# Issuing a batch's four input loads in two pairs, with the residual load and the probability stores between them

## The chip, the core and the metric

The kernel runs on one core of a Trainium2 chip. A core has a matrix engine (TensorE, PE in the profile, with its weight loads as PEld), a vector engine (VectorE, DVE), an activation engine (ScalarE, ACT), a general engine (GpSimd, POOL) and a queue engine (SyncE, SP), each with its own program, in order. They synchronise through semaphores. Transfers between the chip's memory (DRAM) and the on-chip memory run on 16 DMA engines. The metric is the time of one execution on the device in microseconds (us); lower is better.

## The reference, cut to what matters

The input x has 32 batches of 512 queries with 640 channels. The context has 77 keys per batch with 1024 channels. The text keys alone reach the attention that counts; there are 20 heads of 32 channels:

```python
residual = hidden_states
end = N_TXT                                    # 77
ehs_txt = encoder_hidden_states[:, :end]
...
q = _heads(hidden_states @ to_q_w)
h_txt = _sdpa(q, _heads(ehs_txt @ to_k_w), _heads(ehs_txt @ to_v_w))
...
out = _merge(h_txt) + SCALE_OBJ * _merge(h_obj) + SCALE_OTH * _merge(h_oth) + SCALE_IP * _merge(h_ip)
out = out @ to_out_w + to_out_b
out = (out + residual) / RESCALE               # RESCALE is 1
```

The context of this case has exactly 77 rows, so the slices for the object, other and image keys are empty, and their softmax over no keys adds zero. What is left is a cross attention of x to the context, a projection, a bias and the residual x, all in float32.

## The kernel before, in words

Matmuls take their float32 operands as a high and a low part (the high part is a copy in a narrower format, the low part the difference), and run three products: high by high, high by low, low by high. The function `split` and its relatives make the two parts: ScalarE copies, VectorE or GpSimd subtracts.

A first stage (up to line 252) computes all keys and values from the context and stores them in DRAM (`k_dram`, `v_dram`), and the split output weights in `wo_dram`. Then the main part runs 160 *slots*, one for each batch b and each group j = 0..4 of four heads, n = 5b + j. The order of all instructions of the main part is written out by hand (`tc.manual_schedule`), so each engine executes in the order of the program's text. `slot(n)` does, in this order and for quarters t = 0..3 of the queries:

- `refill`: loads of keys or values for later slots, on SP: in j=0 the keys of groups 2 to 4 (L309, L312), in j=1 and j=3 values (L319), in j=2 the next batch's keys.
- `cast_p`, `rest_p`, `last_p`: the probabilities of slot n-3, loaded from DRAM into `raw` one slot earlier, are split on ScalarE (L431, L437), VectorE (L438) and GpSimd (L445) into `pp`.
- `scores(n, t)` on TensorE (L367) with the maximum on VectorE (L375), and `exps(n, t)` on ScalarE (L385).
- `normalize(n-1)`: GpSimd scales the probabilities of the slot before in place (L400), behind the reciprocals of VectorE (L395).
- `queries(n+1)` on TensorE (L332), `split_q(n+1)` on ScalarE (L343, L347) and VectorE (L349).
- `load_p(n-2)` on SP (L423, L424): transposed probabilities back from DRAM into `raw`.
- `transpose_p(n-1)`: VectorE transposes blocks of 32x32 from `pn` into `z` (L407), and SP stores `z` to a DRAM tile `pd` with four transfers (L414). The tile `z` has one buffer, so the transposition of a slot waits until the stores of the slot before have landed.
- `values(n-3)` on TensorE (L459), and two `piece`s of the output projection (L489) of an earlier batch, whose results VectorE adds to bias and residual (`finish`, L517) and SP stores (L521).

Beside that, every batch's x is brought in. `load_x` loads it into the tile `xs`, which has one buffer, by four transfers of 32 partitions each (L267; 512 pieces of 640 bytes). They are issued on SP in slot j=4 of batch b for batch b+2. In slots j=0, 1 and 2 of the next batch VectorE transposes `xs` in place in four parts (`transpose_x`, L272), each of which reads all 128 partitions, so the first needs all four transfers. In slots j=2 and 3 `split_x` makes the parts `xt` of the query matmuls (L279, L280). The residual is loaded a second time, in the layout of the output (`load_residual`, L478), in slots j=1 to 4.

All transfers of the main part are issued by SP in program order. In slot j=4 that order is: two loads into `raw`, four loads of x, one load of the residual, four stores of `z`, one store of the output. Slot j=0 then begins with four loads of keys (kb, kc, kb, kc), two loads into `raw`, four more loads of keys and four stores of `z`.

Of the kernel before, what the change touches and what calls it, by code (L numbers as in the profile page):

```python
# [8 lines left out]
F32 = mybir.dt.float32  # L9
# [14 lines left out]
P = 128  # L24
Q = 32
# [25 lines left out]
def kernel(  # L51
# [26 lines left out]
    B, S, C = x.shape  # L78
# [176 lines left out]
    main = ctx.enter_context(tc.tile_pool(name="main", bufs=1, reuse_waits="tile"))  # L255
# [3 lines left out]

    xts, raws, pps, ats, xss, pds, sms, pqs, pas, xrs, pos = ({} for _ in range(11))  # L260

    def load_x(b):

        xs = main.tile([P, S // Q, C // 4], F32, tag="xs", name="xs")
        src = x[b].rearrange("(a j) (q u) -> q j a u", j=Q, q=4)
        for q in range(4):
            nc.sync.dma_start(xs[q * Q : (q + 1) * Q, :, :], src[q])  # L267
        xss[b] = xs

    def transpose_x(b, i):  # L270
        part = xss[b][:, 4 * i : 4 * i + 4, :].rearrange("p a u -> p (a u)")
        nc.vector.transpose(part, part)  # L272
# [53 lines left out]
    def queries(n, k0, k1):  # L326
        b, j = divmod(n, NC_)
        if k0 == 0:
            pqs[n] = ps.tile([P, S], F32, tag="pq", name="pq", bufs=1)
        for k in range(k0, k1):  # L330
            for m, (a, c) in enumerate(PAIRS):
                nc.tensor.matmul(  # L332
                    pqs[n],
                    wq_s[:, k, a, j * P : (j + 1) * P],
                    xts[b, k][:, c, :],
                    start=(k == 0 and m == 0),
                    stop=(k == NC_ - 1 and m == 2),
                )
# [14 lines left out]
    def scores(n, t):  # L353
        b, j = divmod(n, NC_)
        g = GROUP_OF[j]
        qt, (kb, kc) = qts[n % 2], kbs[g]
        jg = j - GROUPS[g][0]
        sc = ps.tile([P, S], F32, tag="sc", name="sc", bufs=3)
        half = KCOLS // 2
        for m, (cols, keys_) in enumerate(  # L360
            (
                (slice(0, KCOLS), kb[:, jg]),
                (slice(0, half), kc[:, jg, 0]),
                (slice(half, KCOLS), kc[:, jg, 1]),
            )
        ):
            nc.tensor.matmul(  # L367
                sc[:, cols],
                qt[:, m, t * P : (t + 1) * P],
                keys_,  # L370
                start=(m == 0),
                stop=(m == 2),
            )
        nm = main.tile([P, HPC], F32, tag="nm", name="nm", bufs=3)
        nc.vector.tensor_reduce(  # L375
            nm, sc[:, :KCOLS].rearrange("p (h k) -> p h k", k=NKEY), AX.X, ALU.max, negate=True
        )
        return sc, nm

    def exps(n, t, sc, nm):  # L380
        if t == 0:
            sms[n] = main.tile([P, NQ * HPC], F32, tag="sm", name="sm", bufs=2)
        for i in range(HPC):
            at = t * HPC + i
            nc.scalar.activation(  # L385
                pnb[n % 2][:, at, :NKEY],
                sc[:, i * NKEY : (i + 1) * NKEY],
                AF.Exp,
                bias=nm[:, i : i + 1],
                accum_out=sms[n][:, at : at + 1],  # L390
            )

    def sums(n):
        rs = main.tile([P, NQ * HPC], F32, tag="rs", name="rs", bufs=2)
        nc.vector.reciprocal(rs, sms.pop(n))  # L395
        return rs

    def normalize(n, rs):
        pf = pnb[n % 2][:, :, :NKEY]
        nc.gpsimd.tensor_tensor(  # L400
            pf, pf, rs.unsqueeze(2).to_broadcast([P, NQ * HPC, NKEY]), ALU.mult
        )
# [17 lines left out]
    def load_p(n):  # L420
        pd = pds.pop(n)
        raw = late[0].tile([P, 3, S], F32, tag="raw", name="raw", bufs=2)
        nc.sync.dma_start(raw[:, 0:2, :], pd[0 : 2 * P, :].rearrange("(k p) q -> p k q", p=P))  # L423
        nc.sync.dma_start(raw[:64, 2, :], pd[2 * P :, :])  # L424
        raws[n] = raw

    def cast_p(n):

        raw = raws[n]
        pp = late[0].tile([P, 5, S], FPR, tag="pp", name="pp", bufs=1)  # L430
        nc.scalar.copy(pp[:, 0:2, :], raw[:, 0:2, :])  # L431
        pps[n] = pp

    def rest_p(n):

        raw, pp = raws[n], pps[n]
        nc.scalar.copy(pp[:64, 4, :], raw[:64, 2, :])  # L437
        nc.vector.tensor_tensor(  # L438
            pp[:, 2:4, :], raw[:, 0:2, :], pp[:, 0:2, :].bitcast(F32), ALU.subtract
        )  # L440

    def last_p(n):

        raw, pp = raws.pop(n), pps[n]
        nc.gpsimd.tensor_tensor(  # L445
            pp[64:, 4, :], raw[:64, 2, :], pp[:64, 4, :].bitcast(F32), ALU.subtract
        )
# [27 lines left out]
    def load_residual(b, t, xr=None):  # L475
        if xr is None:
            xr = late[0].tile([P, C], F32, tag="xr", name="xr", bufs=3)
        nc.sync.dma_start(xr, x[b, t * P : (t + 1) * P, :])  # L478
        xrs[b, t] = xr

    def add_bias(b, t):
        nc.gpsimd.tensor_tensor(xrs[b, t], xrs[b, t], bias, ALU.add)  # L482
# [28 lines left out]
    def finish():  # L511

        while closed:
            b, t, h = closed.pop(0)
            xr = xrs[b, t]
            cols = slice(h * HALF, (h + 1) * HALF)
            nc.vector.tensor_tensor(  # L517
                xr[:, cols], pos.pop((b, t, h))[:, :HALF], xr[:, cols], ALU.add
            )
            if h == 1:  # L520
                nc.sync.dma_start(out[b, t * P : (t + 1) * P, :], xr)  # L521
# [21 lines left out]
    def refill(b, j, part):  # L543

        heads = range(2 * part, 2 * part + 2)
        segments = SEGMENTS[4 * part : 4 * part + 4]
        if j == 0:
            load_keys(b, 1, heads)
        elif j == 1:
            load_values(b, 0, segments)  # L550
        elif j == 2 and b + 1 < B:
            load_keys(b + 1, 0, heads)
        elif j == 3:
            load_values(b, 1, segments)

    def slot(n, beside=None):
        b, j = divmod(n, NC_)
        ahead, more = n + 1 < N, b + 1 < B
        back, first = PIECES[j]
        bo_, has_out = b - back, b >= back  # L560
        xsplits = SPLIT_X.get(j, ((), ())) if more else ((), ())
        turns = TRANSPOSE_X.get(j, ((), (), ())) if more else ((), (), ())
        taken, second = takes.get(n), seconds.get(n)

        refill(b, j, 0)
        if taken is not None:
            cast_p(taken)
        s = scores(n, 0)
        if taken is not None:
            rest_p(taken)  # L570
        if n:
            normalize(n - 1, sums(n - 1))
        if taken is not None:
            last_p(taken)
        exps(n, 0, *s)
        if ahead:
            queries(n + 1, 0, 2)
        s = scores(n, 1)
        if n - LAG + 1 in pds and n > LATE:
            load_p(n - LAG + 1)  # L580
        refill(b, j, 1)
        finish()
        if j == 4 and b + 2 < B:
            load_x(b + 2)
        if j in RESIDUAL and b >= RESIDUAL[j][0]:
            load_residual(b - RESIDUAL[j][0], RESIDUAL[j][1])
        if j in BIAS and b >= BIAS[j][0]:
            add_bias(b - BIAS[j][0], BIAS[j][1])
        exps(n, 1, *s)
        for i in turns[0]:  # L590
            transpose_x(b + 1, i)
        if ahead:
            queries(n + 1, 2, NC_)
        s = scores(n, 2)
        if n:
            transpose_p(n - 1)
        if ahead:
            split_q(n + 1)
        exps(n, 2, *s)
        for c in xsplits[0]:  # L600
            split_x(b + 1, c)
        if has_out:
            piece(bo_, first)
        if taken is not None:
            values(taken)
        if beside:
            beside()
        s = scores(n, 3)
        finish()
        for i in turns[1]:  # L610
            transpose_x(b + 1, i)
        if taken is not None:
            split_a(taken)
        for c in xsplits[1]:
            split_x(b + 1, c)
        exps(n, 3, *s)
        if has_out:
            piece(bo_, first + 1)
        for i in turns[2]:
            transpose_x(b + 1, i)  # L620
        if second is not None:
            cast_p(second)
            rest_p(second)
            last_p(second)
            take(second)
            if second + 2 in pds and second + 2 not in takes.values():
                load_p(second + 2)
# [141 lines left out]
```

## Time and profile before

| | us |
|---|---|
| three executions | 2025.39, 2026.93, 2027.08; median 2026.93 |
| the profiled execution | 2018.67, of which the span 2016.9 |
| TensorE busy in the span | 1963.4 (97%) |
| ScalarE, VectorE, GpSimd busy | 1588.0 (79%), 1354.7 (67%), 981.9 (49%) |
| DMA: 421.10 MB on SP's queue | 82.4% of the 16 engines' time |
| x loads, issue to landing | 7.5 median, 3.9 to 10.8 |
| z stores (`pd<-z`), issue to landing | 3.6 median |

How to read it: "L407 z" is the instruction of line 407 that writes tile z. In a row of a timeline the first number is the start in us from the span's start, the second the duration, and the brackets give the idle time of the engine before it and what ended that. In a row of waits the numbers are the total in us, how many times, and the longest. In a row of DMA issues they are the number of transfers, the size of one in KB, and the median time from issue to landing. The chain of work goes back from the last instruction, at each step to what released it. Idle time of an engine that isn't on the path to the end costs nothing.

### The profile page before, as it was taken

The page shows a single profiled execution, that of the slowest core. Times are in us where ns is not written, and L with a number is a line of the kernel's source. Part 1 is how long each engine was busy: PE and PEld are TensorE (multiplying, and loading weights), DVE is VectorE, ACT ScalarE, POOL GpSimd, SP SyncE. Part 2 cuts the span into 40 slices and gives each one's busy share as a digit, 9 for nine tenths or more (in the row PEclk, how much of TensorE's full clock was granted, in tenths as well). Part 3 has the DMA queues.
Part 4 walks back from the last instruction along what each step waited for, and adds up shares of the span by engine and source line. Part 5 has one row for each costly group of instructions (what it writes and reads, how often), then busy time and mean ns, then how long its engine had stood idle before and what let it go on. Part 6 is the DMA issues. An engine that isn't in the chain of part 4 may idle for free.

```text
span 2016.9 us, 38271 instructions
## 1 busy us (share of the span) xinstructions
PE 1963.4 (97%) x11012; PEld 1763.5 (87%) x11012; DVE 1354.7 (67%) x2159; ACT 1588.0 (79%) x6377; POOL 981.9 (49%) x617
## 2 busy tenths in 40 slices
PE   9999997899999999999999999999999999999998
PEld 7889986789888988888898888888888888988898
DVE  4443225777777777777777677777777777777764
ACT  3321128889889988888898899899898889989993
POOL 0000023555555555555556555666555655555554
PEclk9999998999999999999999999999999999999999
DMA  7993366888888888888988888888888888888875
GB/s 172 221 255 108 105 148 151 222 222 221 223 223 220 226 218 226 217 218 218 229 226 220 208 227 229 222 223 218 217 222 219 218 224 218 228 222 222 222 202 169
DMA packets 555997, 423.55 MB, mean 210 GB/s; under 512 B 170191, under 2 KB 459501, under 8 KB 555789
## 3 DMA queue, kind: packets, MB, share of 16 engines
q1 hardware_dynamic: 555789, 421.10, 82.4%
q8 instruction: 91, 1.49, 0.3%
q14 instruction: 117, 0.96, 0.1%
HBM read 245.61 MB, written 175.32 MB: 209 GB/s over the span
## 4 chain that ended last, share of the span: by engine, by line
PE 54%; DMA 19%; SPq 8%; POOL 6%; issue 5%; ACT 4%; DVE 4%; DVEq 0%; POOLq 0%; ACTq 0%
PE pq L332 17%; PE po L489 15%; DMA pd<-z 8%; PE pa L459 8%; PE sc L367 6%; POOL pn L400 4%; PE pv L197 4%; PE pk L168 4%; DMA xs<-in_x_dram 3%; DMA raw<-pd 3%; SPq L414 2%; DVE qt L349 2%; ACT pn L385 2%; POOL pp L445 2%; DMA kb<-k_dram 1%
## 5 line engine op out<-in xcount | busy, mean ns | idle before, releaser
L385 ACT ACTIVATE pn<-sc,nm 128x77 f32<-128x77 f32 x2560 | 799.2, 329 | 109.3 <-DVE nm L375 96.5
L400 POOL TENSOR_TENSOR pn<-pn,rs 128x1232 f32<-128x1232 f32 x160 | 364.5, 2278 | 692.6 <-DVE rs L395 541.2
L489 PE MATMUL po<-wo_s,at 128*128 128x320 f32 x3840 | 627.6, 313 | 1.4 <-DVE xr L517 1.4
L332 PE MATMUL pq<-xt,wq_s 128*128 128x512 f32 x2400 | 622.5, 400 | 0.0
L489 PEld LDWEIGHTS po<-wo_s,at 128*128 128x128 f32 x3840 | 567.0, 189 | 2.0 <-DVE xr L517 1.7
L385 ACT ACTIVATION_READ_ACCUMULATOR pn<-sc,nm 128x1 f32 x2560 | 530.6, 207 | 0.0
L332 PEld LDWEIGHTS pq<-xt,wq_s 128*128 128x128 f32 x2400 | 429.7, 190 | 77.5 <-POOL xt L280 0.2
L375 DVE TENSOR_REDUCE nm<-sc 128x4 f32<-128x308 f32 x640 | 294.0, 460 | 264.3 <-PE sc L367 258.1
L459 PE MATMUL pa<-pp,vb 128*128 128x512 f32 x1280 | 337.7, 402 | 19.6 <-ACT pp L431 9.9
L407 DVE STREAM_TRANSPOSE z<-pn 128x1280 f32<-128x1280 f32 x160 | 241.8, 1511 | 119.2 <-DMA pd<-z 62.4
L459 PEld LDWEIGHTS pa<-pp,vb 128*128 128x128 f32 x1280 | 242.5, 197 | 68.3 <-POOL pp L445 20.7
L367 PEld LDWEIGHTS sc<-kc,qt 128*128 128x128 f32 x1280 | 213.3, 189 | 40.9 <-issue 13.9
L367 PE MATMUL sc<-kc,qt 128*128 128x154 f32 x1280 | 227.1, 256 | 13.6 <-DVE qt L349 12.9
L438 DVE TENSOR_TENSOR pp<-raw,pp 128x1024 fp32r<-128x1024 f32 x160 | 196.2, 1226 | 50.1 <-ACT pp L431 34.3
L445 POOL TENSOR_TENSOR pp<-raw,pp 64x512 fp32r<-64x512 f32 x160 | 209.4, 1309 | 36.4 <-ACT pp L437 24.3
L349 DVE TENSOR_TENSOR qt<-pq,qt 64x512 fp32r<-64x512 f32 x320 | 214.3, 670 | 7.5 <-ACT qt L343 3.1
L280 POOL TENSOR_TENSOR xt<-xs,xt 128x512 fp32r<-128x512 f32 x157 | 199.7, 1299 | 16.8 <-ACT xt L279 12.2
L482 POOL TENSOR_TENSOR xr<-xr,bias 128x640 f32<-128x640 f32 x128 | 201.2, 1573 | 12.0 <-POOL pp L445 2.7
L347 ACT CAST qt<-qt 64x512 fp32r<-64x512 f32 x320 | 198.1, 619 | 9.0
L367 PE MATMUL sc<-kb,qt 128*128 128x308 f32 x640 | 196.0, 306 | 1.2 <-ACT qt L343 1.2
L431 ACT CAST pp<-raw 128x1024 fp32r<-128x1024 f32 x160 | 170.1, 1063 | 1.3 <-DVE at L105 0.8
L104 ACT CAST at<-pa 128x512 fp32r<-128x512 f32 x160 | 94.9, 593 | 75.5 <-PE pa L459 72.8
(41 smaller groups left out, 1536.3 us busy)
## 6 DMA issues: line engine op xcount, KB each, us to landing
pd<-z SPq DMA_DIRECT2D x640, 160.0 KB, 3.6
raw<-pd SPq DMA_DIRECT2D x160, 512.0 KB, 4.1
xs<-in_x_dram SPq DMA_DIRECT2D x128, 320.0 KB, 7.5
xr<-in_x_dram SPq DMA_DIRECT2D x128, 320.0 KB, 3.8
out_dram<-xr SPq DMA_DIRECT2D x128, 320.0 KB, 3.3
raw<-pd SPq DMA_DIRECT2D x160, 128.0 KB, 4.2
v_dram<-vs SPq DMA_DIRECT2D x19, 640.0 KB, 4.0
k_dram<-ks SPq DMA_DIRECT2D x80, 128.0 KB, 2.4
```

The lines of the kernel that those rows point to most:

```text
L280: engine.tensor_tensor(parts[1], src, parts[0].bitcast(F32), ALU.subtract)
L332: nc.tensor.matmul(pqs[n], wq_s[:, k, a, j * P : (j + 1) * P], xts[b, k][:, c, :], start=(k == 0 and m == 0), stop=(k == NC_ - 1 and m == 2),)
L349: nc.vector.tensor_tensor(qt[r, 1 + w, :], pq[r], qt[r, 0, :].bitcast(F32), ALU.subtract)
L367: nc.tensor.matmul(sc[:, cols], qt[:, m, t * P : (t + 1) * P], keys_, start=(m == 0), stop=(m == 2),)
L375: nc.vector.tensor_reduce(nm, sc[:, :KCOLS].rearrange("p (h k) -> p h k", k=NKEY), AX.X, ALU.max, negate=True)
L385: nc.scalar.activation(pnb[n % 2][:, at, :NKEY], sc[:, i * NKEY : (i + 1) * NKEY], AF.Exp, bias=nm[:, i : i + 1], accum_out=sms[n][:, at : ...
L400: nc.gpsimd.tensor_tensor(pf, pf, rs.unsqueeze(2).to_broadcast([P, NQ * HPC, NKEY]), ALU.mult)
L407: nc.vector.transpose(z.rearrange("p b t j -> p t b j"), pn.rearrange("p (t h) k -> p t (h k)", t=NQ).rearrange("p t (b i) -> p t b i", i=Q),)
L445: nc.gpsimd.tensor_tensor(pp[64:, 4, :], raw[:64, 2, :], pp[:64, 4, :].bitcast(F32), ALU.subtract)
L459: nc.tensor.matmul(pas[n], vb[:, t, :, a], pp[:, c, :], start=(m == 0), stop=(m == len(PASSES) - 1),)
L482: nc.gpsimd.tensor_tensor(xrs[b, t], xrs[b, t], bias, ALU.add)
L489: nc.tensor.matmul(pos[b, t, h][:, :HALF], ats[b * NC_ + j][:, a, t * P : (t + 1) * P], wos[0][:, j, c, h * HALF : (h + 1) * HALF], start= ...
```

## The change

`load_x` gets an argument that says which of the four quarters are to be loaded, and makes the tile at the first call. In slot j=4 the first two quarters are loaded where all four were; the other two after `exps(n, 2)`. In SP's queue the order of slot j=4 becomes: two loads into `raw`, two loads of x, the residual's load, four stores of `z`, two loads of x, the output's store. The loads of x of the first two batches, ahead of the slots, stay as they are. Sizes, buffers and all other instructions are the same.

```diff
-    def load_x(b):
-
-        xs = main.tile([P, S // Q, C // 4], F32, tag="xs", name="xs")
+    def load_x(b, quarters=range(4)):
+
+        if b not in xss:
+            xss[b] = main.tile([P, S // Q, C // 4], F32, tag="xs", name="xs")
+        xs = xss[b]
         src = x[b].rearrange("(a j) (q u) -> q j a u", j=Q, q=4)
-        for q in range(4):
+        for q in quarters:
             nc.sync.dma_start(xs[q * Q : (q + 1) * Q, :, :], src[q])
-        xss[b] = xs
...
         refill(b, j, 1)
         finish()
         if j == 4 and b + 2 < B:
-            load_x(b + 2)
+            load_x(b + 2, (0, 1))
         if j in RESIDUAL and b >= RESIDUAL[j][0]:
             load_residual(b - RESIDUAL[j][0], RESIDUAL[j][1])
...
         exps(n, 2, *s)
+        if j == 4 and b + 2 < B:
+            load_x(b + 2, (2, 3))
         for c in xsplits[0]:
             split_x(b + 1, c)
```

## The prediction

> **What bounds the kernel now.** I read the page's shares first, then the waits, then the chain for the length of single slots, then one batch in the timelines of the engines and of SP's queue, and last that batch's transfers. Page, sections 1 and 3:
>
> ```profile
> PE 1963.4 (97%) x11012; PEld 1763.5 (87%) x11012; DVE 1354.7 (67%) x2159; ACT 1588.0 (79%) x6377; POOL 981.9 (49%) x617
> q1 hardware_dynamic: 555789, 421.10, 82.4%
> ```
>
> TensorE is the bound; the transfers, all of them issued by SP, fill 82% of the DMA engines' time. So a gain can only come from TensorE's own stalls. The waits from 500 to 1950 us (27.6 batches), TensorE's and VectorE's:
>
> ```profile
> PE sc L367 <- DVE qt L349: 8.1, 22, 0.8
> PE pa L459 <- POOL pp L445: 5.9, 22, 0.8
> DVE z L407 <- DMA pd<-z: 60.9, 22, 4.0
> ```
>
> TensorE has two stalls in most batches, and VectorE has one wait on DMA in most, at the block transposition into z. The idle times understate TensorE's loss, because the ends of matmuls are modelled and a pipeline that stalls must refill. The length of a slot tells it better. In the chain of work the x6 rows are the first query matmuls of five slots in a row:
>
> ```profile
> 857.53 1.43 PE pq L332 x6
> ...
> 867.86 1.43 PE pq L332 x6
> ...
> 878.19 1.43 PE pq L332 x6
> ...
> 888.75 1.43 PE pq L332 x6
> ...
> 899.59 0.50 PE pq L332 x2
> ```
>
> Slots j=3 and j=4 take 10.33 us each, j=0 takes 10.56, j=1 takes 10.84. The same distances over the whole trace: j=2, 3, 4 take 10.31, 10.33, 10.32 in nearly every batch; j=0 and j=1 take 10.79 each in the mean and 10.31 at their shortest. A batch takes 52.57 us in the mean against an unstalled 51.59. Over the 29 batches from the third to the last but one the losses add up to **28.5 us**, half in j=0 and half in j=1. That is the most that anything can return here, bar the startup.
>
> The same batch on VectorE, GpSimd and ScalarE, from slot j=4 (transposition at 872.77, my zero below) to j=1:
>
> ```profile
> 872.77 1.51 DVE L407 STREAM_TRANSPOSE z<-pn 128x1280 f32<-128x1280 f32 x1 [0.19 <-POOL pn L400]
> ...
> 882.42 0.48 DVE L375 TENSOR_REDUCE nm<-sc 128x4 f32<-128x308 f32 x1 [1.78 <-PE sc L367]
> 885.49 1.51 DVE L407 STREAM_TRANSPOSE z<-pn 128x1280 f32<-128x1280 f32 x1 [2.59 <-DMA pd<-z]
> 886.92 1.37 DVE L349 TENSOR_TENSOR qt<-pq,qt 64x512 fp32r<-64x512 f32 x2
> ...
> 889.25 0.83 DVE L272 STREAM_TRANSPOSE xs<-xs 128x640 f32<-128x640 f32 x1
> ```
>
> z has one buffer, so the transposition in j=0 waits until the four stores of j=4's z have landed. VectorE was ready at 882.90 and started 2.59 us late; behind it the lower halves of the queries (L349) end at 888.29, while TensorE's scores want them at 888.01. After that VectorE runs without a pause to 892.7, and GpSimd's scaling and subtraction, behind it, release the last two values matmuls of j=1 only at 896.39 instead of about 895.7. Both stalls hang on that store. SP's queue:
>
> ```profile
> 870.70 2.57 SPq L267 DMA_DIRECT2D xs<-in_x_dram  x4
> 873.32 1.35 SPq L478 DMA_DIRECT2D xr<-in_x_dram  x1
> 874.71 3.71 SPq L414 DMA_DIRECT2D pd<-z  x4
> ...
> 885.44 0.38 SPq L423 DMA_DIRECT2D raw<-pd  x1
> ```
>
> The stores are issued behind four x loads and the residual. The DMA view of this batch, for the fourth x load alone, the fourth store alone, and the next slot's first probability load:
>
> ```profile
> xs<-in_x_dram SPq DMA_DIRECT2D x1, 320.0 KB, 9.2
> ...
> pd<-z SPq DMA_DIRECT2D x1, 160.0 KB, 8.0
> ...
> raw<-pd SPq DMA_DIRECT2D x1, 512.0 KB, 4.5
> ```
>
> Issue plus landing time, load by load: x at 876.4, 878.2, 879.8, 881.6 (1.7 us apart), residual at 883.5, stores at 884.0, 884.4, 884.9, 885.3. A store takes 3.6 us over the whole run, here 8.0 to 9.3.
>
> **The change part by part.**
>
> *The stores go past two x loads.* Nothing is added or removed: twelve transfers, the same bytes, in another order. Two loads fewer ahead of the stores take 2 × 1.7 = 3.4 us off the last store's landing: 885.3 becomes 881.9. Can they be issued early enough? The transposition ends at 874.28; four issues of some 0.6 us end near 877, and 4.9 us to landing is above the usual 3.6. So VectorE's transposition starts at 882.9, when it is ready, 2.6 us earlier; the query halves end at 885.7, 2.3 us before TensorE asks. The stall in j=0 goes. Bounds: nothing gained if the stores land as late as now, all of j=0's loss (about 14 us) if they land by 884.5. Across the batches the last store lands 11.3 to 13.9 us after zero, the forecast is 7.9 to 10.5, and VectorE is ready at 10.1; I take all of it.
>
> *The Trainium skill against this, first place.* In the rows the nine transfers land in the order of issue. The page "DMA: Bandwidth & Descriptors", section "Queues, rings and completion order", says that completion is not first-in first-out per issuing engine; were that to rule here, an earlier place in the queue would buy no earlier landing, and the sum would be zero instead of 3.4 us per batch on the store. The rows show the order kept, and I go by them.
>
> *Stall in j=1.* Its release is a chain: probability load lands, ScalarE casts (890.06), VectorE subtracts (891.15), sums, GpSimd 892.68 to 896.33. From landing (885.44 + 4.5 = 889.9) to TensorE that is 6.4 us, and VectorE's lateness is a second condition. The first condition alone, with VectorE freed and the load landing as now, would keep 12 of the 28.5 us: I laid the batches over one another, the load lands 15.7 to 18.9 us after zero, and each us past 16.6 is lost. Does the load land earlier? It is issued when the stores have landed, so it moves from 885.4 to about 882. Ahead of it in the queue stand the second x pair, the output store and four small key loads, the same bytes as before, which were through at 886.8. In the DMA view's slices of 0.5 us from 885.5 on the engines moved 21, 13, 90 and 229 GB/s, a hole, because the load had only just been issued; it closes. 512 KB at the 400 GB/s shown for such loads take 1.3 us, so it lands at 888.1, 1.8 us earlier. Bounds: 889.9 (as now) and 887.4 (1.3 us behind the output store's landing at 886.1). I take 888.1, as the bytes ahead are known. Only the latest batches then stay past 16.6.
>
> *The second pair goes past the residual and the stores.* It lands after the stores: 881.9 + 3.4 = 885.3 for the last quarter, 3.7 us later than now. All four quarters are needed by the first x transposition (L272 in j=0), now at 889.25. With VectorE freed it can start after the maximum of j=0's last scores (TensorE 885.89, maximum and output sum until 887.5): 2.2 us to spare. Cost nothing; the cover is VectorE's work up to 887.5 and, behind it, about 1.5 us that the chain to the values matmuls can lose. Without cover it would cost TensorE 1 us per us.
>
> *The skill, second place.* Landing 881.6 against use at 889.25 is 7.7 us of slack. The same page, section "Rules for kernel authors", says to issue a DMA early and wait on its semaphore late, which speaks against moving loads back. By that rule the step is a loss of up to 3.7 us of cover per batch; by the rows it is 3.7 of 7.7 us, a loss of zero.
>
> *SP's own waits.* Key loads at the top of j=0 wait 31 times each for x loads issued eight transfers before (L312 42.6 us, L309 16.0 us in SP's waits): an issue is held until the eighth before it has landed. In the new order these places hold the residual and the stores, which land earlier; the second pair itself stands eight behind the last probability load and the first x load, landed at 874.7 and 876.4, as the pair is issued near 877. The key loads serve slots j=2 on, so they cost nothing either way. The output store is issued a little earlier or the same; nobody waits for it. The residual lands 3.4 us earlier and is used in the next slot. SP issues every transfer of the main part, so no other engine's queue is passed.
>
> **Sum.** 28.5 us, less 0.1 us per batch kept for late transfers (a few batches pass with 0.1 or less lost now): 28.5 − 2.9 = 25.6. The startup's own stall (slot 4, a probability load of 6.4 us wait) has its transfers ahead of the x loads, so no change. The profiled execution took 2018.67 us (span 2016.9, 1.8 around it), so it would take 1993. The shown median, 2026.93, is 8.3 us above the profiled one; I take the gain off the median: **2001.3 us**.
>
> **The rivals.**
> 1. *Half.* The stores land early, the probability load does not (the loads behind fill the hole with something else). Then 12 us stay, gain 16.5: 2010. For it: DMA at 82%. Against: the idle stretch at 886.
> 2. *No change.* The landing order does not follow the queue, or SP's issues of the stores are held so that they land as now: 2027. Against: the rows above.
> 3. *Slower.* The second x pair comes late, and VectorE waits at L272 with everything behind it. It decides from a landing at about 890 (17 after zero) on, 5 us later than forecast: from there TensorE loses more than now. Landing at 891 loses 1 us more than now in each of 29 batches: 2056. For it: two more places behind four stores. Against: the bytes ahead are counted, and they are three x loads short of this.
>
> **How the numbers follow.** Full gain 0.66 (1996 to 2006: nothing kept for late transfers gives 1998, and 2 us for the spread of the runs), half 0.20 (2006 to 2018, about its 2010), no change 0.06, slower 0.08. A measurement tells 0.2% (4 us) from nothing. Faster 0.86, same 0.06, slower 0.08. For 8 in 10 I take the first two cases: 1996 to 2018.
>
> **What would show it.** Right: the wait of z for DMA gone from VectorE, slots j=0 and j=1 at 10.31 us, the last store landing about 8 to 10 us after zero, last x quarter about 12.5. Wrong: a wait of L272 on DMA, or slot j=1 still long with ScalarE's cast right behind the load's landing.

## The result, and the profile after

| | before | after |
|---|---|---|
| median of the executions, us | 2026.16 (2023.31 to 2027.08) | 1999.55 (1996.0 to 2002.37) |
| the profiled execution, us | 2018.67 (span 2016.9) | 1996.0 (span 1994.2) |
| ratio | | 0.987, 95% interval 0.9851 to 0.9889 |

The changed kernel is faster by 1.3%, which is 22 to 30 us. The page after, shares of the engines and of SP's queue:

```profile
PE 1950.5 (98%) x11012; PEld 1760.0 (88%) x11012; DVE 1352.5 (68%) x2159; ACT 1598.2 (80%) x6377; POOL 982.8 (49%) x617
...
q1 hardware_dynamic: 555789, 421.10, 83.9%
```

TensorE does the same 11012 matmuls in 22.7 us less span. The waits from 500 to 1930 us, of TensorE, VectorE and ScalarE (a line of the code is now one to three further down; L408 is the transposition into z, L446 GpSimd's subtraction, L432 ScalarE's cast of the probabilities):

```profile
PE pa L460 <- POOL pp L446: 4.5, 7, 1.5
...
DVE z L408 <- DMA pd<-z: 2.0, 5, 0.7
...
ACT pp L432 <- DMA raw<-pd: 25.8, 23, 2.2
```

TensorE's wait for the query halves is gone from the list, and its wait for the values' operand is down from 22 times to 7 (5.9 to 4.5 us). VectorE waits 2.0 us for z's stores where it waited 60.9. In their place ScalarE now waits for the probability load, 23 times. The chain's query matmuls in the same batch as before:

```profile
857.73 1.42 PE pq L333 x6
...
868.05 1.43 PE pq L333 x6
...
878.36 1.44 PE pq L333 x6
...
888.70 1.43 PE pq L333 x6
...
899.00 1.43 PE pq L333 x6
```

Slots j=4, 0, 1 and 2 take 10.32, 10.31, 10.34 and 10.30 us: no slot of this batch loses anything. Over the 29 batches from the third to the last but one j=0 takes 10.309 us every time, j=1 takes 10.62 in the mean, with 10.335 as median and 12.15 at most. The loss over these batches is 8.9 us (28.5 before), all of it in j=1. SP's queue and VectorE in this batch, zero (the transposition in j=4) at 862.65:

```profile
861.02 1.07 SPq L269 DMA_DIRECT2D xs<-in_x_dram  x2
862.14 0.48 SPq L479 DMA_DIRECT2D xr<-in_x_dram  x1
864.19 2.43 SPq L415 DMA_DIRECT2D pd<-z  x4
866.66 1.75 SPq L269 DMA_DIRECT2D xs<-in_x_dram  x2
...
872.64 0.39 SPq L424 DMA_DIRECT2D raw<-pd  x1
```

```profile
872.28 0.48 DVE L376 TENSOR_REDUCE nm<-sc 128x4 f32<-128x308 f32 x1 [1.77 <-PE sc L368]
872.67 1.50 DVE L408 STREAM_TRANSPOSE z<-pn 128x1280 f32<-128x1280 f32 x1
...
877.19 0.84 DVE L273 STREAM_TRANSPOSE xs<-xs 128x640 f32<-128x640 f32 x1
```

The transposition starts 10.0 us after zero with no idle time before it (12.7 and 2.59 us of idling before the change), and the transposition of x waits for nothing.

In all numbers of landings below, "after zero" is a median over 28 batches of one execution, counted from the start of the transposition in slot j=4; "loss" is the time by which the batches' slots exceed 51.59 us, added up over 29 batches.

| order in SP's queue | z stores landed | last x quarter | probability load of j=0 | loss, us |
|---|---|---|---|---|
| before | 12.7 | 9.5 | 16.9 | 28.5 |
| changed | 9.4 | 12.5 | 16.4 | 8.9 |

Batch by batch, both stalls follow a threshold. Before the change 19 of the 28 batches lost more than 0.05 us in j=0, and each lost the time by which z's transposition started past 12.45 us after zero, to within 0.02 us; the others started by 12.46 and lost 0.01 us at most. In the changed kernel 13 of 28 batches lost time in j=1, 0.15 to 1.82 us, and each lost the time by which the probability load landed past 16.45, again to within 0.02 us; in the other 15 it had landed by 16.43 and nothing was lost.

### The profile page after: what moved, and what is told of

It reads as the page before. It is cut to its first block, busy times and chain, and to the rows that moved or that the text cites. A ratio compares the mean times of both kernels' runs of the same rounds, so it can differ in the third digit from the quotient of the medians.

```text
span 1994.2 us, 38184 instructions
## 1 busy us (share of the span) xinstructions
PE 1950.5 (98%) x11012; PEld 1760.0 (88%) x11012; DVE 1352.5 (68%) x2159; ACT 1598.2 (80%) x6377; POOL 982.8 (49%) x617
## 4 chain that ended last, share of the span: by engine, by line
PE 78%; DMA 9%; SPq 4%; POOL 3%; ACT 2%; issue 2%; DVE 2%; DVEq 0%; ACTq 0%; POOLq 0%
PE po L490 24%; PE pq L333 24%; PE pa L460 13%; PE sc L368 9%; PE pv L197 4%; PE pk L168 4%; DMA raw<-pd 3%; POOL pn L401 2%; DMA pd<-z 2%; SPq L114 1%; DMA xs<-in_x_dram 1%; POOL pp L446 1%; ACT pn L386 1%; DMA k_dram<-ks 1%; DMA cs<-in_ctx_dram 1%
## 5 line engine op out<-in xcount | busy, mean ns | idle before, releaser
L408 DVE STREAM_TRANSPOSE z<-pn 128x1280 f32<-128x1280 f32 x160 | 241.5, 1509 | 36.2 <-POOL pn L401 31.6
L446 POOL TENSOR_TENSOR pp<-raw,pp 64x512 fp32r<-64x512 f32 x160 | 209.4, 1309 | 37.0 <-ACT pp L438 19.8
L368 PE MATMUL sc<-kc,qt 128*128 128x154 f32 x1280 | 222.9, 255 | 4.5 <-DVE qt L350 3.9
L281 POOL TENSOR_TENSOR xt<-xs,xt 128x512 fp32r<-128x512 f32 x157 | 200.0, 1296 | 19.4 <-ACT xt L280 12.5
L432 ACT CAST pp<-raw 128x1024 fp32r<-128x1024 f32 x160 | 170.1, 1063 | 29.7 <-DMA raw<-pd 28.9
```

The source lines that it names most:

```text
L281: engine.tensor_tensor(parts[1], src, parts[0].bitcast(F32), ALU.subtract)
L368: nc.tensor.matmul(sc[:, cols], qt[:, m, t * P : (t + 1) * P], keys_, start=(m == 0), stop=(m == 2),)
L408: nc.vector.transpose(z.rearrange("p b t j -> p t b j"), pn.rearrange("p (t h) k -> p t (h k)", t=NQ).rearrange("p t (b i) -> p t b i", i=Q),)
L446: nc.gpsimd.tensor_tensor(pp[64:, 4, :], raw[:64, 2, :], pp[:64, 4, :].bitcast(F32), ALU.subtract)
```

## The experiments

Each edit is shown against the changed kernel. The quarters of x are numbered 0 to 3.

**How much has to pass?** Three quarters ahead, one behind:

```diff
-            load_x(b + 2, (0, 1))
+            load_x(b + 2, (0, 1, 2))
...
-            load_x(b + 2, (2, 3))
+            load_x(b + 2, (3,))
```

> Three x quarters stay ahead of the residual and the z stores, one goes behind them. Theory (the wait of z for its stores is what cost, and it costs only when it ends later than about 12.4 us after the transposition of slot j=4): the last store lands about 1.7 us later than in the changed kernel, 11.1 us after zero, z in j=0 starts near 11.2, no loss in j=0, slot j=1 loses as in the changed kernel or a little more (8 to 12 us in 29 batches): 1999 to 2005 us. Rival (the gain goes with the bytes taken from ahead of the stores): half of the gain, about 2013 us.

1993.56 us, ratio 0.9849 (0.9832 to 0.9865). The stores landed 10.1 after zero, the transposition started at 10.2, j=0 took 10.32. With a single quarter moved all but 0.4 us of j=0's loss (15.0 before) was gone: it is not the bytes moved that pay but the end of one wait. The loss in all was 3.1 us, where 8 to 12 in j=1 alone were expected: the probability load landed at 15.2, past 16.5 in only 5 of 28 batches. Why it lands earlier here than in the changed kernel, no run shows by itself.

And no quarter ahead, four behind:

```diff
-        if j == 4 and b + 2 < B:
-            load_x(b + 2, (0, 1))
...
-            load_x(b + 2, (2, 3))
+            load_x(b + 2)
```

> All four x quarters go behind the residual and the z stores. Theory: the stores land 3.4 us earlier still, about 6 us after zero, but VectorE is ready for z only at 10.0, and all bytes ahead of the probability load of slot j=0 are the same, so it lands at the same 16.4 and the last x quarter at the same 12.5: the changed kernel's time within 2 us. Rival one (earlier stores go on paying): 5 to 10 us faster than the changed kernel. Rival two (loads should be issued early): the transposition of x waits, slower than the changed kernel.

2034.79 us, ratio 1.0063 (1.0039 to 1.0086): slower than before the change, which the theory had not said. Half of it held: the stores landed at 6.6, z waited for nothing, j=0 took 10.309. But j=1 took 11.77 in the mean, a loss of 42 us. It was not the transposition of x that waited (it started at 14.55, as in the changed kernel), so the second rival has the right sign and the wrong place. ScalarE shows it, in its waits from 500 to 1960 us and in the batch with zero at 881.99:

```profile
ACT pp L432 <- DMA raw<-pd: 64.2, 27, 3.9
```

```profile
900.04 1.05 ACT L432 CAST pp<-raw 128x1024 fp32r<-128x1024 f32 x1 [2.56 <-DMA raw<-pd]
```

The probability load landed at 17.6 instead of 16.4, and the last x quarter at 13.7 instead of 12.5. The same bytes lay ahead of it; they took longer. The DMA view of 20 us from 2.7 us ahead of zero, the changed kernel first, then this one:

```profile
DMA packets 6542, 4.73 MB, mean 237 GB/s; under 512 B 1540, under 2 KB 5634, under 8 KB 6540
```

```profile
DMA packets 5391, 4.21 MB, mean 211 GB/s; under 512 B 1168, under 2 KB 4496, under 8 KB 5389
```

In these two batches half a megabyte less went through; in the mean over 28 batches it is a quarter of one (4.65 against 4.42 MB), and before the change it was 4.43, so the sum alone settles nothing. The landings show where the time went. From the landing ahead of them to the last store's, the residual and the four stores took 4.3 us, where they take 2.6 in the changed kernel and 2.8 before the change; the four x loads took 6.9 to 7.1 us in all three. Until 1.5 us after zero the stores wait for the transposition, and here no x load is queued for that time. Then the four stores, with only the residual ahead of them, land 0.6 to 1.1 us apart (3.96, 4.93, 5.54, 6.61), where they land 0.4 to 0.7 apart before the change; and the x loads are not issued before 3.9 us after zero. So the loads ahead of the stores do useful work: the DMA engines move them in the time in which the stores aren't ready. That this order of work makes the load late is read from these rows; no run changed the filling alone with all else equal.

**What sets the rest, in slot j=1?** In the changed kernel the cast begins 0.08 us behind the landing of the probability load in 25 of 28 batches, so the load is what is late. Two runs tried to bring it forward by issuing less ahead of it. First the four key loads of slot j=0 behind it:

```diff
-        refill(b, j, 0)
+        if j:
+            refill(b, j, 0)
...
             load_p(n - LAG + 1)
+        if j == 0:
+            refill(b, j, 0)
         refill(b, j, 1)
```

> The changed kernel, and in slot j=0 the first four key loads are issued behind the two probability loads instead of ahead of them. Theory (what is left in slot j=1, 8 us over the batches, is the landing of the probability load, held by the bytes ahead of it): the load lands 1 us or so earlier (15.4 instead of 16.4 after zero), the loss of j=1 falls to 2 or 3 us, 5 to 6 us faster than the changed kernel. Rival (the small key loads do not delay it, or VectorE's or GpSimd's work is what is late): no change against the changed kernel, within 1 us.

2041.17 us, ratio 1.0072 (1.0045 to 1.0099): neither theory nor rival, but a new loss of 54 us, now in j=2 and j=3 too (10.58 and 10.60 us). The load landed at 17.0, not 15.4. SP's queue in slot j=0 (zero at 881.71), and VectorE's waits from 500 to 1970 us:

```profile
892.36 0.39 SPq L424 DMA_DIRECT2D raw<-pd  x1
...
895.86 0.43 SPq L313 DMA_DIRECT2D kc<-k_dram  x1
897.87 0.30 SPq L310 DMA_DIRECT2D kb<-k_dram  x1
898.44 1.20 SPq L313 DMA_DIRECT2D kc<-k_dram  x1
899.74 2.31 SPq L415 DMA_DIRECT2D pd<-z  x4
```

```profile
DVE z L408 <- DMA pd<-z: 103.2, 72, 3.2
```

The load waits in SP's queue for the stores of j=4, and everything behind it waits with it. The key loads, which could have been issued in that time, come after it; the last two of them stand eight places behind the probability loads and are held until these have landed (897.86 and 898.42, added from issue and time to landing), and behind them stand the stores of slot j=0. Those are issued 18 us after zero instead of 14.7, land at 22.7 instead of 19.8, and the transposition of the next slot waits, and so on round: 72 waits for stores in the place of 5. Over 28 batches the two probability loads landed at 16.95 and 17.38 after zero, and the last two key loads were issued at 16.96 and 17.43; in none of the 13 traces of this study is a transfer of the main part issued before the eighth ahead of it has landed. So the hold itself is shown; that it causes the new loss is read from the waits, as it was not taken away in a run of its own.

Then the output store of slot j=4 (320 KB), held back until the probability loads of j=0 have been issued:

```diff
-            if h == 1:
+            if h == 1 and hold:
+                held.append((b, t, xr))
+            elif h == 1:
                 nc.sync.dma_start(out[b, t * P : (t + 1) * P, :], xr)
...
         s = scores(n, 3)
-        finish()
+        finish(j == 4 and more)
...
             load_p(n - LAG + 1)
+        while held:
+            ob, ot, oxr = held.pop()
+            nc.sync.dma_start(out[ob, ot * P : (ot + 1) * P, :], oxr)
```

> The changed kernel with the output store of slot j=4 issued behind the probability loads of slot j=0, so that 320 KB less lie ahead of them. Theory (the load lands late for the bytes ahead of it): it lands about 0.8 us earlier, the loss of slot j=1 falls to 3 or 4 us, 4 to 5 us faster. Rival (the order of single transfers does not set it): within 1 us of the changed kernel.

1997.51 us, ratio 0.9854 (0.9829 to 0.9879), beside 1998.71 for the changed kernel on the same chip: no difference that the measurement shows. The load landed at 16.6 after zero, no earlier, and the loss was 6.8 us, not 3 or 4. So the time is the rival's. But the landings don't bear out its reason. The whole queue ran later than in the changed kernel's first run: slot j=4's own probability load, ahead of the place of the edit, landed at 2.6 instead of 1.65, the stores of j=4 at 10.1 instead of 9.4, the second x pair at 13.5 instead of 12.5. Behind that pair the load landed after 2.8 us, where it takes 3.9 and 4.1 in the two runs of the changed kernel. So 320 KB less ahead of it brought the load about 1.1 us nearer, where the theory had 0.8, and the later queue took that away. Why the queue ran later is open.

The changed kernel and the one with one quarter behind ran again beside these:

> The changed kernel once more, beside the next three: 1994 to 2002 us, slot j=1 the only one that loses, 6 to 11 us in 29 batches.

1998.71 us, ratio 0.9866 (0.9844 to 0.9888). The load landed at 15.7 and the loss was 9.7 us, 3.6 of them in one batch: from run to run the landing moves by some 0.7 us.

> Three x quarters ahead of the stores, one behind, once more. If it is really better than the changed kernel (its loss in slot j=1 was about 3 us against 9, as the probability load of slot j=0 landed at 15.2 instead of 16.4 us after zero), it is 4 to 7 us faster than that here; if the first run was a lucky one, the two are within 2 us.

1996.61 us, ratio 0.9859 (0.9835 to 0.9883), loss 2.4 us, load at 15.1. The loss in the slots is smaller again, by 7 us, but the difference of the medians, 2 us, lies inside the spread of the runs: better in the trace, not shown to be better in the time.

**The idle stretch instead of the passing.** Ahead of slot j=4's own probability loads SP waits for the stores of j=3, and the DMA engines stand nearly idle (28 GB/s at its lowest in the mean over the batches, 2 us ahead of zero, before the change). Quarter 0 put there:

```diff
+        if j == 4 and b + 2 < B:
+            load_x(b + 2, (0,))
         if n - LAG + 1 in pds and n > LATE:
             load_p(n - LAG + 1)
...
-            load_x(b + 2, (0, 1))
+            load_x(b + 2, (1,))
```

> The changed kernel with the first x quarter moved ahead of slot j=4's own probability loads, where the DMA engines stood nearly idle for about 1.5 us because these loads wait for stores. Theory (DMA time is what is short between slots j=4 and j=1, and idle stretches are the reserve): everything behind lands about 1 us earlier, the loss of slot j=1 falls from 8 to 2 or 3 us: 5 us faster than the changed kernel. Rival (the probability load of slot j=4, now behind a quarter, comes late for its cast in slot j=0): a new loss in j=0, no faster or slower than the changed kernel.

1993.16 us, ratio 0.9834 (0.9813 to 0.9855), 5.5 us below the changed kernel on the same chip. The probability load of j=0 landed at 15.0, the loss was 3.0 us, 1.3 of it in the first of the 29 batches. ScalarE's waits for it from 500 to 1900 us, 25.8 us in the changed kernel:

```profile
ACT pp L432 <- DMA raw<-pd: 7.9, 9, 1.9
```

The load of slot j=4, now behind a quarter, landed at 2.3 instead of 1.6, and j=0 still took 10.309: it had that much to spare.

The same early quarter with nothing moved behind the stores, so that the stores pass no load of x:

```diff
-            load_x(b + 2, (0, 1))
+            load_x(b + 2, (1, 2, 3))
...
-            load_x(b + 2, (2, 3))
```

(and quarter 0 as above)

> The kernel before, with the first x quarter alone moved ahead of slot j=4's probability loads; the other three stay ahead of the residual and the stores, nothing goes behind them. Theory (what counts is when the stores and the next probability load land, not that they pass the x loads; the idle stretch of the DMA engines is as good): the last store lands at about 11.3 us after zero, z in j=0 starts there, no loss in j=0, the probability load near 15.5 to 16.5, slot j=1 loses 3 to 8 us in 29 batches: 1994 to 2002 us. Rival (stores must pass loads, the bytes ahead of them decide): like the kernel before, 2015 us or more.

2002.73 us, ratio 0.9889 (0.9875 to 0.9902). The stores landed at 11.8 (forecast 11.3), the loss was 11.9 us, 5.0 of it in j=0, where none was expected. Most of the change's gain comes without the change's own order, by an earlier landing of the stores (11.8 for 12.7) and of the load behind them (16.1 for 16.9): the theory of the landing, not of the passing. In j=0 only batches whose z started past about 12.4 lost time, as the trace of before had it.

Both together, and the early quarter once more:

```diff
+        if j == 4 and b + 2 < B:
+            load_x(b + 2, (0,))
         if n - LAG + 1 in pds and n > LATE:
             load_p(n - LAG + 1)
...
-            load_x(b + 2, (0, 1))
+            load_x(b + 2, (1, 2))
...
-            load_x(b + 2, (2, 3))
+            load_x(b + 2, (3,))
```

> First x quarter ahead of slot j=4's probability loads, two ahead of the residual and the stores, one behind: the two best orders so far together. Theory (slots j=0 and j=1 have at most 3 us left to give in 29 batches): within 2 us of the kernel with the first quarter early and two behind. Rival (idle time and passing add up): another 3 us or more.

1989.16 us, ratio 0.9822 (0.9809 to 0.9836), loss 0.6 us.

> First x quarter early, one ahead, two behind, once more beside the other two: ratio to the kernel before 0.982 to 0.985, loss of slot j=1 1 to 3 us.

1990.46 us, ratio 0.9831 (0.9817 to 0.9844), loss 0.6 us. The two are within 2 us of each other, as the theory had it: there is nothing left for them to take in these slots, all of j=0 to 4 run at TensorE's own pace. Both are faster than the kernel before, and by their ratios to it (0.9822 and 0.9831) faster than the changed one (0.987 and 0.9866), which did not run beside them.

**What does lateness of x cost?** The second pair moved on into slot j=0, behind its probability and key loads:

```diff
-        if j == 4 and b + 2 < B:
-            load_x(b + 2, (2, 3))
...
         refill(b, j, 1)
+        if j == 0 and b and b + 1 < B:
+            load_x(b + 1, (2, 3))
```

> The second pair of x loads goes still further back, into slot j=0 behind its probability loads and eight key loads. Theory (the rival of lateness has its threshold where the prediction put it): the probability load lands near 13, the last x quarter near 17.5 us after zero, the first transposition of x waits for it on VectorE from 14.5 on, and slot j=1 loses 1.5 to 2 us per batch: 2035 to 2055 us, slower than before the change. Rival (VectorE has more slack than that, x may come late at no cost): as fast as the changed kernel or up to 8 us faster, as the probability load is early.

2044.2 us, ratio 1.0107 (1.0087 to 1.0127), as the theory had it. VectorE's waits from 500 to 1970 us, and the batch with zero at 883.71:

```profile
DVE xs L273 <- DMA xs<-in_x_dram: 70.2, 26, 3.7
```

```profile
900.98 0.84 DVE L273 STREAM_TRANSPOSE xs<-xs 128x640 f32<-128x640 f32 x1 [2.64 <-DMA xs<-in_x_dram]
```

The last quarter landed at 17.2 and the first transposition of x started at 17.4 after zero; j=1 lost 1.46 us in the median; 25 of 28 batches lost the time by which that start lay past 15.94, to within 0.03 us. The probability load landed at 12.4, its earliest in any run, and did not help: TensorE now waited for VectorE.

## Why the prediction was right

The forecast was 2001.3 us, the measurement 1999.55. Point by point:

- *The stores go past two x loads: right, in mechanism and size.* Last store at 9.4 after zero (forecast 9.1 for the batch shown, 7.9 to 10.5 over the batches), transposition at 10.03 when VectorE is ready, j=0 at its shortest in every batch. The single-quarter run and the early-quarter run show that what decides is whether the landing lets z start by 12.45 after zero.
- *The skill's sentence on completion order* in "DMA: Bandwidth & Descriptors", section "Queues, rings and completion order", did not come into play: in none of the 13 traces did a transfer of the main part land ahead of one issued before it. The sentence speaks of an order that isn't guaranteed; that an earlier place in the queue would then buy nothing, as the forecast put it, is more than it says.
- *The stall in j=1: mechanism right, term mis-sized.* The forecast let the probability load land 1.8 us earlier, so that only the latest batches would stay past 16.6, and kept 2.9 us of loss. The condition held: each us past 16.45 cost 1 us. But the load landed only 0.5 us earlier (16.9 to 16.4; 15.7 in the second profile), 13 of 28 batches stayed late, and 8.9 us of loss stayed. In these batches one of the forecast's own signs of being wrong came true, ScalarE's cast right behind the landing of the load. Two sizes were off. The bytes ahead of the load were through at 14.5 after zero, where the batch of the forecast had 14.0; and the load then took 1.8 us, not 1.3. I had taken a rate of 400 GB/s from slices in which the load had the engines for itself; here small key loads and stores were queued behind it, but that they made it slower is not shown. The step that failed is that the same bytes ahead take the same time, and the run with all quarters behind shows how far it can fail: there they took 1.2 us longer again.
- *The second pair: cost nothing, right.* Last quarter at 12.5 (forecast 12.5), the transposition of x at 14.54 without a wait. The forecast said free until about 1.5 us beyond 887.5, which is 16.2 after zero, and then 1 us per us. The late pair bears out the rate and puts the threshold at 15.94: it started its transposition at 17.36 and lost 1.46.
- *The skill's rule to issue early and wait late* ("Rules for kernel authors" on the same page): against the changed order the rows won, since the slack was used and nothing lost. But the rule has its part: the fastest kernels here issue one quarter earlier than before, into an idle stretch (and one or two later), and the one that put all four later was slower.
- *SP's own waits: nothing, right* in the changed kernel. The second probability load is now held for the third x quarter, which the forecast didn't name (issued at 11.17, when that quarter had landed at 11.15); it still landed 0.3 us behind the first. These waits are not harmless in general, as the run with the key loads behind showed.
- *The sum fits better than its terms.* The losses in the slots fell by 19.6 us, not 25.6. The profiled pair of executions differs by 22.7: 3.6 us of that lie ahead of the first query matmul (293.1 against 289.4 us), in a stage that the change does not touch and that took 289 to 296 us in the runs of this study. The medians differ by 26.6. So some 6 us too much were forecast for the slots, and the spread of the runs put about as much back: that forecast and measurement meet within 2 us is luck.

## What to carry to other kernels

When several transfers share one in-order queue, find for each the time at which it is needed, and put the ones with slack behind a store whose landing frees a buffer that the critical engine's work waits for; here 3 of the 7.7 us of slack in an input load bought 2.7 us at a transposition and with them two stalls of TensorE per batch. But don't move everything back: while a store is not ready yet, the DMA engines have work only if something with slack stands ahead of it. Here two or three of four loads ahead beat both four and none. Then look for stretches in which the queue waits and the engines are idle, and put a transfer with slack there.

## What was not expected

- Putting all four x loads behind the stores moved less in 20 us than the changed kernel (4.42 against 4.65 MB in the mean over 28 batches) and made the kernel 0.6% slower than before the change, although the store that everything hung on landed 6 us earlier.
- Four stores of 160 KB with only the residual ahead of them landed 0.6 to 1.1 us apart; before the change, behind queued loads, 0.4 to 0.7 us apart.
- In every trace here an issue of SP is held until the eighth transfer before it has landed. Moving four key loads of 29 to 58 KB by two places held up the stores of z by 3 us and cost 0.7% against the kernel before, 2% against the changed one.
